# A polynomial in place of theta's logarithm on GpSimd, and memory-layer work cut into halves with second places in the order

## The chip, the cores and the metric

The kernel runs on one core of a Trainium2 chip. The core has five engines that matter here: TensorE (PE, matrix products; its weight loads are shown as PEld), VectorE (DVE), ScalarE (ACT), GpSimd (POOL) and SyncE (SP, which issues the transfers). The metric is the device time of one execution in microseconds, as the median of several runs.

## The reference

The input `x` is four sequences of 1024 rows of 256 numbers, in float32. Four layers follow each other, each added to what went in:

```python
x = x + attention(layernorm(x))      # 16 heads of 16, a second norm inside, softmax over 1024 keys
x = x + ffn(layernorm(x))            # one 256x256 product with weights of -1, 0, 1 times a scale
x = x + memory_layer(layernorm(x))
x = x + ffn(layernorm(x))
```

The memory layer makes keys, values and queries of width 64 by products and a causal convolution over four rows, and three numbers per row from the same input: alpha, eta (means of sigmoids) and theta, `(softplus(hidden @ tW.T + tb) * 0.1).mean(-1)`. Softplus is log(1 + exp(x)), computed here as max(x, 0) + log(1 + exp(-|x|)). In chunks of 128 rows, the gradient of a small two-layer network's loss is taken for each row at the state at the chunk's start, clipped in its norm, and two recurrences run over the rows, `S = eta * S - theta * g` and `W = (1 - alpha) * W + S`. What the network answers with each row's own `W` is multiplied with `Wo`, divided by the root of its mean square, and gated.

## The kernel before

**Blocks and units.** The attention runs over the queries in four blocks of 256 rows. Each block has eight units (a sequence and half of the heads), 32 in all, numbered u. A unit goes through eight turns, one for each 128 keys; the text writes turn 10.4 for the turn with the fifth keys of unit 10. A turn has two half-steps (`half`, with `pr` 0 and 1). In a half-step TensorE computes four matmuls of row maxima (`mx`, L244), for a unit ten turns ahead, then eight of scores (`sc`, L284) and two that subtract the maxima (L292). VectorE reduces `mx` (`nm`, L249) and ScalarE takes two exps of the scores (`pt`, L298). `weigh` (L312) multiplies the exps of the turn before with the values.

**PSUM.** `mx` has two buffers, the sums one, and the scores and every tile of side work share a ring of three (`mps`).

**Side work in lanes.** Everything else that can run beside the attention is a generator in one of the lanes settle, finish, theta, memory, ready, answers, last, outputs, before. `finish` makes the attention's output, its norm, and the first ffn of a pair of tiles (`po`, `hn`, `pf`, `hd`). When all tiles of a block are through, `theta` is started for each chunk of the block (two chunks), and `memory()` runs `prepare` (convolutions, eta, alpha, scans), `advance` (the gradient and the state) and `retrieve` (the answers) of the chunk, then starts `output` (product with `Wo`, gate, norm, last ffn, store). A generator yields where others may come between; the number that it yields is the time until it may go on, in turns of the written order (a half-step counts 0.5). `beside` is called once a turn, after the first half-step, and takes pieces from the lanes as long as a budget of TensorE columns lasts.

**What sets the order.** The order of TensorE, VectorE and ScalarE is the order in which the program emits the instructions, up to `by_hand.close()` behind the last unit. GpSimd's and SyncE's order is set by a scheduler, as is all of the tail (`rest`, `alone`), in which the last block's theta, memory layer and outputs run. An engine works through its own order and stands at an instruction whose input isn't there.

**Names that the change touches.** `theta`: `u` is exp(-|x|) (L507), the logarithm is the activation at L512, with the rounding of 1 + u put right by L509, L510 and a subtraction on GpSimd (L513); `thp` is the product that takes the mean. `prepare`: `vkps` and `qqps` are the projections (L559), `convolved` the convolution with one ScalarE and three VectorE operations, `natp` the transposed keys and values and `nat` their copy, the square of `nat` on GpSimd (L591, in the buffer named `ms`), `kk` its sum on VectorE (L596), `aeps`, `pa` and `pe` the numbers eta and alpha, L621 and L642 the scans on VectorE, `kqp` the product of keys and queries (L651) and `kqm` (L653) and `qq` (L654) what is made of it. `advance`: `zT`, `zn`, `prT`, `prn`, `da` are products of the gradient. `output`: `gps` the gate, `ops` the product with `Wo`, `o2` its copy, then squares, a reciprocal root (`rsi_o`, `rso_o`), the gating, the sum into `X`, statistics and norm of the result (`rsi_e`, `rso_e`, `nb_e`), the transposition `oth` and the last product `opf`. A norm is applied on ScalarE (L91), from a reciprocal root on GpSimd (L72) and a shift there (L84, L85).

In `output` the test `add is not V.tensor_add` holds in every call, since each access to `V.tensor_add` makes a new object: the last chunk's call takes the same branches as the others.

Of the kernel before, what the change touches and what calls it, by code (L numbers as in the profile page):

```python
# [13 lines left out]
ALU = mybir.AluOpType  # L14
# [12 lines left out]
D = 64  # L27
N5 = 512
EPS_LN = 1e-5

OWN = {mybir.EngineType.PE, mybir.EngineType.DVE, mybir.EngineType.Activation}

# [5 lines left out]
def tile_hybrid(ctx: ExitStack, tc: tile.TileContext, x, ln_gamma, ln_beta, w_qkv, b_qkv, w_out, b_out,  # L38
# [63 lines left out]
    def flat(t):  # L102
        return t.rearrange("p b t -> p (b t)")
# [350 lines left out]
    )}  # L454
    at = {"now": 0.0, "due": 0}

    def start(lane, gen, key=None):
        lanes[lane].append([gen, at["now"], key])

    def piece(lane):  # L460

        w = lanes[lane][0]
        n = taken[0]
        gap = next(w[0], None)
        used = taken[0] - n
        at["now"] += used / 1500
        if gap is None:
            lanes[lane].pop(0)
        else:
            w[1] = at["now"] + gap  # L470
        return used

    def beside(pace):

        at["due"] = min(at["due"] + pace, 1500)
        done = 0
        for lane in lanes:
            while lanes[lane] and lanes[lane][0][1] <= at["now"] and at["due"] >= 1 and done < 700:
                used = piece(lane)
                at["due"] -= used  # L480
                done += used
        return done

    def alone():

# [10 lines left out]
    def theta(k, cs):  # L496


        xh = xs_of[k][:, cs].rearrange("p c b t -> p (c b t)")
        m = cs.stop - cs.start  # L500
        u, w = (
            pools["lp"].tile([P, N5 // 2], F32, tag=f"th{name}", name=f"{name}_{k}_{cs.start}")[:, : 2 * m * P]
            for name in "uw"
        )
        V.scalar_tensor_tensor(out=u, in0=xh, scalar=-1.0, in1=xh, op0=ALU.mult, op1=ALU.min)
        yield 1
        A.activation(u, u, AF.Exp)  # L507
        yield 1
        V.tensor_scalar(w, u, 1.0, None, ALU.add)  # L509
        V.scalar_tensor_tensor(out=u, in0=w, scalar=-1.0, in1=u, op0=ALU.add, op1=ALU.subtract)  # L510
        yield 1
        A.activation(w, w, AF.Ln)  # L512
        G.tensor_sub(w, w, u)  # L513
        yield 1
        V.scalar_tensor_tensor(out=w, in0=xh, scalar=0.0, in1=w, op0=ALU.max, op1=ALU.add)
        yield 2
        ps = mps([P, m, 2, 2], f"thp_{k}_{cs.start}", 256)
        for c in range(m):
            for b in range(2):
                o = (2 * c + b) * P  # L520
                T.matmul(ps[:, c, :, b], lhsT=w[:, o : o + P], rhs=ot, start=True, stop=True)


        c0 = BLOCKS[k][0] // P + cs.start
        V.tensor_scalar(thn[:, c0 : c0 + m, :], ps.rearrange("p c h b -> p c (h b)"), -0.01, None, ALU.mult)
        yield 1
# [23 lines left out]
    def prepare(c, g, own):  # L550
# [12 lines left out]
        def convolved(what, w, cw):  # L563
            ps = projected(w, f"{what}ps")
            r = wk.tile([P, B, P + 3], F32, tag="w", name=f"r{what}_{c}")
            if c == 0:
                G.memset(r[:, :, 0:3], 0.0)
            else:
                G.tensor_copy(r[:, :, 0:3], carry[what])
            A.copy(r[:, :, 3:], ps)  # L570
            carry[what] = small.tile([P, B, 3], F32, tag=f"cy{what}", name=f"cy{what}_{c}", bufs=2)
            G.tensor_copy(carry[what], r[:, :, P : P + 3])
            y = own(what)
            A.activation(y, r[:, :, 0:P], AF.Identity, scale=cw[:, 0:1], bias=cw[:, 4:5])
            for j in range(1, 4):
                V.scalar_tensor_tensor(
                    out=y, in0=r[:, :, j : j + P], scalar=cw[:, j : j + 1], in1=y, op0=ALU.mult, op1=ALU.add
                )
            g[what] = y
            return y  # L580

        vk = convolved("vk", wvk, cw_vk)
        yield 1

        ps = mps(full, f"natp_{c}", 256)
# [5 lines left out]
        G.tensor_mul(sq, nat[:, :, D:], nat[:, :, D:])  # L591
        g["nat"] = nat
        yield 0
        qq = convolved("qq", wqq, cw_qq)
        kk = small.tile([P, B], F32, tag="kk", name=f"kk_{c}")
        V.tensor_reduce(kk, sq, AX.X, ALU.add)  # L596
        g["kk"] = kk
# [20 lines left out]
        V.memset(oma[:, :, 0:1], 0.0)  # L618

        def scan(dst, factor, added, r=slice(0, P)):  # L620
            V.tensor_tensor_scan(  # L621
                out=flat(dst)[r, :], data0=flat(factor)[r, :], data1=flat(added)[r, :], initial=0.0,
                op0=ALU.mult, op1=ALU.add,
            )

        scan(x1, eta, fe, slice(0, D))
        yield 1
        au1 = own("au1")  # L630
        scan(au1, oma, x1)
        au2 = own("au2")
        nc.sync.dma_start(au2[:D], au1[D:])
        nc.sync.dma_start(au2[D:], au1[:D])
        el = els[c % 2]
        with nc.allow_non_contiguous_dma(reason="a column"):
            nc.sync.dma_start(el[D:, :], x1[:D, :, P - 1])
        yield 1

        ls = own("dzw")  # L640
        for b in range(B):
            V.tensor_tensor_scan(  # L642
                out=ls[:, b, :], data0=eta[:, b, :], data1=ident, initial=0.0, op0=ALU.mult, op1=ALU.add
            )
        yield 1
        ms = own("ms")
        scan(ms, oma, ls)

        ps = mps(full, f"kqp_{c}", 560)
        for b in range(B):  # L650
# [174 lines left out]
    def output(c, box, groups, op, add):  # L825
# [23 lines left out]
        for p in pairs:  # L849
            ps = mps([P, 2, C], f"ops_{c}_{p.start}", 512)  # L850
            for e in range(2):
                T.matmul(ps[:, e, :], lhsT=ret[:, p.start + e, :], rhs=woT, start=True, stop=True)  # L852
            A.copy(o2[:, p, :], ps)
            for b in (p.start, p.start + 1):
                junk = pools["op"].tile([P, C], F32, tag="hT", name=f"junk_{c}_{b}")
                A.activation(junk, o2[:, b, :], AF.Square, accum_out=ss[:, b : b + 1])
            if p is pairs[1]:
                box.pop(("ret", c))
            yield 0
# [4 lines left out]
        for q in groups:  # L864
            for b in range(q.start, q.stop):
                o = b - q.start
                V.scalar_tensor_tensor(  # L867
                    out=gt[:, b, :], in0=o2[:, b, :], scalar=r[q.start][:, o : o + 1], in1=gt[:, b, :],
                    op0=ALU.mult, op1=ALU.mult,
                )  # L870
            add(X[:, q, c, :], X[:, q, c, :], gt[:, q, :])  # L871
            if add is not V.tensor_add:
                yield 2
            rn[q.start] = norm_stats([X[:, b, c, :] for b in range(q.start, q.stop)], q.stop - q.start, f"e{c}_{q.start}")
            yield 1
# [117 lines left out]
    with ExitStack() as by_hand:  # L993
        by_hand.enter_context(tc.manual_schedule(engines=OWN))
        share(m=8)
        with ExitStack() as s1_:
# [261 lines left out]
            def unit(u):  # L1258
                nonlocal late
                for kc in range(NT):  # L1260
                    if kc == 0:
                        load_keys(u + 1, range(1, 4))
                    if kc == 3:
                        if u + 2 < n0:
                            through("before", lambda key: key <= units[u + 2][1])
                        load_queries(u + 2)
                        load_keys(u + 2, (0,))
                        if u + 1 < U:
                            load_values(u + 1)
# [17 lines left out]
            def memory():  # L1287
                for k, (t0, w) in enumerate(BLOCKS[:-1]):
# [4 lines left out]
                    for c in range(c0, c1):  # L1293
# [11 lines left out]
            def rest():  # L1305
# [52 lines left out]
                start("ready", ready())  # L1358
                for c in cs:
                    if c + 1 < NT:  # L1360
                        start("outputs", output(c, box, [slice(0, B)], to_put(c), G.tensor_add))
# [93 lines left out]
```

## Time and profile before

| | |
|---|---|
| runs | 1477.01, 1477.69, 1477.88 us; median 1477.69 |
| the profiled execution's own time | 1477.84 us |
| its span | 1476.1 us |
| attention with the memory layer beside it | 457.6 to 1342.5 us, 884.9 us |
| tail | 1342.5 to 1476.1 us, 133.6 us |
| instructions on VectorE / ScalarE / GpSimd / SyncE, as built | 1642 / 1448 / 437 / 882 |

The profile is of one execution. A busy share near 1 with a granted clock (PEclk) below 1 means that TensorE works, but slower. Lines of a timeline give the start, the duration, the engine, the line of the program, the operation, out<-in with shapes, how many instructions are taken together, and in brackets the idle time before and what ended it. A group's line ends with busy time and mean duration in ns, then the idle time before and its releasers.

### The profile page before, as it was taken

The page shows a single profiled execution, that of the slowest core. Times are in us where ns is not written, and L with a number is a line of the kernel's source. Part 1 is how long each engine was busy: PE and PEld are TensorE (multiplying, and loading weights), DVE is VectorE, ACT ScalarE, POOL GpSimd, SP SyncE. Part 2 cuts the span into 40 slices and gives each one's busy share as a digit, 9 for nine tenths or more (in the row PEclk, how much of TensorE's full clock was granted, in tenths as well). Part 3 has the DMA queues.
Part 4 walks back from the last instruction along what each step waited for, and adds up shares of the span by engine and source line. Part 5 has one row for each costly group of instructions (what it writes and reads, how often), then busy time and mean ns, then how long its engine had stood idle before and what let it go on. Part 6 is the DMA issues. An engine that isn't in the chain of part 4 may idle for free. (4 is left out here: it accounts for less than half of the span.)

```text
span 1476.1 us, 32993 instructions
## 1 busy us (share of the span) xinstructions
PE 1356.1 (92%) x13568; PEld 843.4 (57%) x13568; DVE 1020.5 (69%) x1640; ACT 785.9 (53%) x1477; POOL 236.8 (16%) x432
## 2 busy tenths in 40 slices
PE   6589999999999999999998999999999999996886
PEld 4346555556555556565654565666556656664664
DVE  5766767587777766877778767776778677712653
ACT  2124636466666555656566655655665555553333
POOL 4431111000000200211011101210102102201232
PEclk9759989999999789999999999999999899988877
DMA  6605432533333221222233222223232022101000
GB/s 219 203 32 197 142 135 81 199 103 109 106 101 112 81 60 59 65 76 84 90 101 109 76 84 77 86 77 98 77 126 80 17 76 90 49 23 37 22 8 29
DMA packets 98211, 132.71 MB, mean 90 GB/s; under 512 B 27980, under 2 KB 70284, under 8 KB 98060
## 3 DMA queue, kind: packets, MB, share of 16 engines
q1 hardware_dynamic: 97788, 129.81, 27.6%
q8 instruction: 107, 1.75, 0.5%
q10 hardware_dynamic: 272, 0.79, 0.1%
q14 instruction: 44, 0.36, 0.1%
HBM read 89.69 MB, written 38.76 MB: 87 GB/s over the span
## 5 line engine op out<-in xcount | busy, mean ns | idle before, releaser
L298 ACT ACTIVATE pt<-sc 128x512 f32<-128x512 f32 x1024 | 555.2, 594 | 452.2 <-PE sc L292 451.6
L249 DVE TENSOR_REDUCE nm<-mx 128x2 f32<-128x1024 f32 x512 | 617.8, 1220 | 144.1 <-PE mx L244 126.1
L284 PE MATMUL sc<-q0slot,kslot 32*128 32x256 f32 x2048 | 373.4, 339 | 24.2 <-ACT pt L298 12.8
L312 PE MATMUL av<-pt,v 128*32 128x256 f32 x4096 | 310.6, 404 | 6.9 <-DVE a L320 6.2
L284 PE MATMUL sc<-q1slot,kslot 32*128 32x256 f32 x2048 | 309.7, 291 | 0.0
L244 PE MATMUL mx<-kslot,q0slot 32*128 32x512 f32 x1024 | 264.8, 516 | 24.3 <-DVE lo L1160 14.0
L284 PEld LDWEIGHTS sc<-q0slot,kslot 32*128 32x128 f32 x2048 | 239.1, 191 | 51.0 <-ACT pt L298 25.4
L244 PEld LDWEIGHTS mx<-kslot,q0slot 32*128 32x128 f32 x1024 | 98.2, 189 | 241.0 <-issue 117.2
L292 PE MATMUL sc<-mslot,ones_r 32*128 32x512 f32 x1024 | 232.5, 405 | 1.8 <-DMA mslot<-d 1.8
L284 PEld LDWEIGHTS sc<-q1slot,kslot 32*128 32x128 f32 x2048 | 233.8, 193 | 0.0
L244 PE MATMUL mx<-kslot,q1slot 32*128 32x512 f32 x1024 | 217.0, 422 | 0.0
L312 PEld LDWEIGHTS av<-pt,v 128*32 128x32 f32 x4096 | 99.2, 111 | 126.9 <-issue 88.8
L292 PEld LDWEIGHTS sc<-mslot,ones_r 32*128 32x128 f32 x1024 | 124.1, 193 | 2.5 <-DMA mslot<-d 2.4
L244 PEld LDWEIGHTS mx<-kslot,q1slot 32*128 32x128 f32 x1024 | 101.2, 195 | 0.0
L1155 PE MATMUL cps<-hT,wg 128*128 128x512 f32 x128 | 61.4, 626 | 0.0
L1160 DVE SCALAR_TENSOR_TENSOR lo<-cps,bqk,hi 128x512 fp32r<-128x512 f32 x32 | 23.9, 751 | 53.4 <-ACT hi L1159 45.4
L1159 ACT ACTIVATE hi<-cps,bqk 128x512 fp32r<-128x512 f32 x32 | 22.0, 687 | 49.9 <-PE cps L1155 24.8
L72 POOL TENSOR_TENSOR rso_hn<-rsi_hn,nhalf 128x2 f32<-128x2 f32 (+1 forms) x17 | 12.0, 708 | 223.1 <-DVE rsi_hn L71 196.8
L72 POOL TENSOR_TENSOR rso_hd<-rsi_hd,nhalf 128x2 f32<-128x2 f32 (+1 forms) x17 | 12.0, 703 | 187.4 <-DVE rsi_hd L71 170.1
L893 PE MATMUL opf<-ffn,ohT 128*128 128x256 f32 x128 | 35.1, 422 | 6.6 <-ACT ohT L888 6.6
L1155 PEld LDWEIGHTS cps<-hT,wg 128*128 128x128 f32 x128 | 24.3, 200 | 28.8 <-issue 26.6
L1196 POOL TENSOR_SCALAR X<-X,rr_a 128x256 f32<-128x256 f32 x32 | 18.5, 588 | 124.4 <-DVE h L1138 124.4
(361 smaller groups left out, 1662.4 us busy)
## 6 DMA issues: line engine op xcount, KB each, us to landing
kslot<-dk SPq DMA_DIRECT2D x64, 512.0 KB
v<-dv SPq DMA_DIRECT2D x32, 604.0 KB
q1slot<-dq SPq DMA_DIRECT2D x128, 64.0 KB
q0slot<-dq SPq DMA_DIRECT2D x64, 128.0 KB
da<-a SPq DMA_DIRECT2D x31, 256.0 KB
dv<-vtile SPq DMA_DIRECT2D x8, 604.0 KB
X<-in_L_attn_a_x_dram SPq DMA_DIRECT2D x8, 512.0 KB
dq<-hi SPq DMA_DIRECT2D x16, 256.0 KB
```

Of the source, the lines that this page charges most:

```text
L72: G.tensor_tensor(out=r[:, :n], in0=t[:, :n], in1=nhalf[:, :n], op=ALU.pow)
L244: T.matmul(ps[:, e, :], lhsT=qS[u][p][o : o + SL, j * P : (j + 1) * P], rhs=kt[o : o + SL, hf * N5 : (hf + 1) * N5], start=p == 0, stop=p ...
L249: V.tensor_reduce(nms[u][:, hf, 2 * pr : 2 * pr + 2, j], ps, AX.X, ALU.max, negate=True)
L284: T.matmul(ps[e][:, g * w : (g + 1) * w], lhsT=kS[u, g][o : o + SL, kc * P : (kc + 1) * P], rhs=qS[u][p][o : o + SL, g * w : (g + 1) * w], ...
L292: T.matmul(ps[e], lhsT=ones[o : o + SL, :], rhs=mslots[u % 2][o : o + SL, :], start=False, stop=True, skip_group_check=True,)
L298: A.activation(pt[:, e, :], ps[e], AF.Exp, scale=1.0 / HD**0.5)
L312: T.matmul(avs[u][SL * i : SL * (i + 1), part * w : (part + 1) * w], lhsT=v[:, kc, o : o + SL], rhs=pts[u, kc, i // 2][:, i % 2, part * w ...
L893: T.matmul(pf[:, e, :], lhsT=hT[:, cc, e, :], rhs=ffn[:, cc, :], start=cc == 0, stop=cc == 1)
L1155: T.matmul(ps, lhsT=wg[:, cc, n * P : (n + 1) * P], rhs=hT[:, cc, o], start=cc == 0, stop=cc == 1)
L1159: A.activation(high, ps, AF.Identity, bias=bqk[:, n : n + 1])
L1160: V.scalar_tensor_tensor(out=low, in0=ps, scalar=bqk[:, n : n + 1], in1=high.bitcast(F32), op0=ALU.add, op1=ALU.subtract,)
L1196: G.tensor_scalar(Xt, Xt, r[:, 6, t : t + 1], r[:, 7, t : t + 1], ALU.mult, ALU.add)
```

## The change

Three things are changed. In `theta`, for all but the last block, log(1 + u) is a polynomial of tenth degree without a constant term, evaluated on GpSimd in 18 operations in place, in three pieces, half a turn apart. In `prepare`, the convolutions and the scans are cut in two, and the second half may follow at a new place: a generator that yields a `Light` number may go on after a turn's second half-step, through `beside_light`, if it adds nothing to TensorE. In `output`, every chunk handles its four sequences in two groups of two, with squares, statistics and norms at separate places, and stores each group by itself.

As built, the counts of instructions become 1666 / 1432 / 574 / 889; TensorE's 10541 matrix instructions stay. On GpSimd, the polynomial of a block's first chunk stands ahead of the square of `nat` (L591), and that of its second chunk, with two of the outer products `al` (L548) in it, ahead of the reciprocal root and shift of `hd` (L72, L84, L85). On VectorE, the two halves of each scan follow one another in the same place. `kqp` and `zT` are in one place in all six chunks beside the attention.

```diff
+LOG1P = (
+    1.0, -0.49999904, 0.33330004, -0.24954559, 0.19678117, -0.15311863, 0.10614265, -0.0570642, 0.01990716, -0.00325638
+)
...
+    class Light(float):
+        pass
+
     def start(lane, gen, key=None):
-        lanes[lane].append([gen, at["now"], key])
+        lanes[lane].append([gen, at["now"], key, False])
...
         else:
-            w[1] = at["now"] + gap
+            w[1], w[3] = at["now"] + gap, isinstance(gap, Light)
         return used
...
+    def beside_light():
+
+        for lane, w in lanes.items():
+            if w and w[0][3] and w[0][1] <= at["now"]:
+                assert piece(lane) == 0
...
         A.activation(u, u, AF.Exp)
         yield 1
-        V.tensor_scalar(w, u, 1.0, None, ALU.add)
-        V.scalar_tensor_tensor(out=u, in0=w, scalar=-1.0, in1=u, op0=ALU.add, op1=ALU.subtract)
-        yield 1
-        A.activation(w, w, AF.Ln)
-        G.tensor_sub(w, w, u)
-        yield 1
+        if k == len(BLOCKS) - 1:
...
+        else:
+            G.tensor_scalar(w, u, LOG1P[-1], LOG1P[-2], ALU.mult, ALU.add)
+            for n, c in enumerate(LOG1P[-3::-1]):
+                G.tensor_mul(w, w, u)
+                G.tensor_scalar(w, w, c, None, ALU.add)
+                if n % 3 == 2:
+                    yield 0.5
+            G.tensor_mul(w, w, u)
+            yield 1
         V.scalar_tensor_tensor(out=w, in0=xh, scalar=0.0, in1=w, op0=ALU.max, op1=ALU.add)
...
             for j in range(1, 4):
+                if j == 2:
+                    yield Light(0)
                 V.scalar_tensor_tensor(
...
-        vk = convolved("vk", wvk, cw_vk)
+        vk = yield from convolved("vk", wvk, cw_vk)
...
-        qq = convolved("qq", wqq, cw_qq)
+        qq = yield from convolved("qq", wqq, cw_qq)
...
         def scan(dst, factor, added, r=slice(0, P)):
-            V.tensor_tensor_scan(
-                out=flat(dst)[r, :], data0=flat(factor)[r, :], data1=flat(added)[r, :], initial=0.0,
-                op0=ALU.mult, op1=ALU.add,
-            )
+            for o in (slice(0, 2), slice(2, 4)):
+                if o.start:
+                    yield Light(0)
+                V.tensor_tensor_scan(
+                    out=flat(dst[:, o])[r, :], data0=flat(factor[:, o])[r, :], data1=flat(added[:, o])[r, :],
+                    initial=0.0, op0=ALU.mult, op1=ALU.add,
+                )
...
-        scan(x1, eta, fe, slice(0, D))
+        yield from scan(x1, eta, fe, slice(0, D))
         yield 1
         au1 = own("au1")
-        scan(au1, oma, x1)
+        yield from scan(au1, oma, x1)
...
-        yield 1
+        yield 0.5
 
         ls = own("dzw")
         for b in range(B):
+            if b == 2:
+                yield Light(0)
             V.tensor_tensor_scan(
...
         ms = own("ms")
-        scan(ms, oma, ls)
+        yield from scan(ms, oma, ls)
+        yield 0
...
             A.copy(o2[:, p, :], ps)
+            if add is not V.tensor_add:
+                yield Light(0.5)
             for b in (p.start, p.start + 1):
...
             add(X[:, q, c, :], X[:, q, c, :], gt[:, q, :])
             if add is not V.tensor_add:
-                yield 2
+                yield Light(1.5)
             rn[q.start] = norm_stats([X[:, b, c, :] for b in range(q.start, q.stop)], q.stop - q.start, f"e{c}_{q.start}")
-            yield 1
+            yield 1 if add is V.tensor_add or q is groups[-1] else Light(0.5)
         for q in groups:
-            (norm_apply_here if q.start else norm_apply)(
+            (norm_apply_here if q.start and add is V.tensor_add else norm_apply)(
...
-            yield 2 if q is groups[-1] and add is not V.tensor_add else 0
+            if add is not V.tensor_add:
+                yield Light(0.5) if q is groups[0] else 2
+            else:
+                yield 0
...
+                        if pr == 1:
+                            beside_light()
...
-                        start("outputs", output(c, box, [slice(0, B)], to_put(c), G.tensor_add))
+                        start("outputs", output(c, box, [slice(0, 2), slice(2, 4)], to_put(c), G.tensor_add))
```

The last edit is made in `memory` and in `rest`.

More of the change, by code (lines that the diff above doesn't have):

```diff
@@ L508, in theta @@
         yield 1
-        V.tensor_scalar(w, u, 1.0, None, ALU.add)
-        V.scalar_tensor_tensor(out=u, in0=w, scalar=-1.0, in1=u, op0=ALU.add, op1=ALU.subtract)
-        yield 1
-        A.activation(w, w, AF.Ln)
-        G.tensor_sub(w, w, u)
-        yield 1
+        if k == len(BLOCKS) - 1:
+            V.tensor_scalar(w, u, 1.0, None, ALU.add)
+            V.scalar_tensor_tensor(out=u, in0=w, scalar=-1.0, in1=u, op0=ALU.add, op1=ALU.subtract)
+            yield 1
+            A.activation(w, w, AF.Ln)
+            G.tensor_sub(w, w, u)
+            yield 1
+        else:
[6 more added lines that the diff above has]
+            G.tensor_mul(w, w, u)
+            yield 1
         V.scalar_tensor_tensor(out=w, in0=xh, scalar=0.0, in1=w, op0=ALU.max, op1=ALU.add)
@@ L1360, in rest @@
                     if c + 1 < NT:
-                        start("outputs", output(c, box, [slice(0, B)], to_put(c), G.tensor_add))
+                        start("outputs", output(c, box, [slice(0, 2), slice(2, 4)], to_put(c), G.tensor_add))
                     else:
```

## The prediction

> **What bounds the kernel now.** I read the page's busy table first, then the clock row of its slices, the groups by shape, the timeline of ScalarE and GpSimd around the logarithm, and stretches of the span. TensorE is the bound; what can be won in the attention is its idle time and its half clock.
>
> ```profile
> PE 1356.1 (92%) x13568; PEld 843.4 (57%) x13568; DVE 1020.5 (69%) x1640; ACT 785.9 (53%) x1477; POOL 236.8 (16%) x432
> PEclk9759989999999789999999999999999899988877
> 457.60:1342.50 884.90, 841.92 (x9077) 529.66 (x9074) 630.51 (x959) 522.07 (x986) 123.80 (x229) 0.95 0.25 78
> 1342.50:1476.10 133.60, 98.59 (x448) 70.71 (x444) 67.13 (x165) 44.62 (x90) 39.51 (x61) 0.78 0.08 22
> ```
>
> The last two rows are stretches: start and end, length, busy time of TensorE, its weight loads, VectorE, ScalarE and GpSimd with counts, granted clock, DMA share, GB/s. The first is the attention with the memory layer beside it, the second the tail. TensorE is busy 95% of the first at a clock of 0.95, GpSimd 14%.
>
> ScalarE's timeline shows what a step costs, and what the logarithm costs:
>
> ```profile
> 342.78 1.09 ACT L298 ACTIVATE pt<-sc 128x512 f32<-128x512 f32 x2 [0.52 <-PE sc L292]
> 344.38 1.09 ACT L298 ACTIVATE pt<-sc 128x512 f32<-128x512 f32 x2 [0.51 <-PE sc L292]
> ...
> 481.91 1.28 ACT L512 ACT_TABLE_LOAD   x1
> 483.20 0.42 ACT L512 ACTIVATE w<-w 128x256 f32<-128x256 f32 x1
> 485.76 1.28 ACT L298 ACT_TABLE_LOAD   x1 [0.99 <-PE sc L292]
> 487.06 1.08 ACT L298 ACTIVATE pt<-sc 128x512 f32<-128x512 f32 x2
> 489.44 1.08 ACT L298 ACTIVATE pt<-sc 128x512 f32<-128x512 f32 x2 [1.30 <-PE sc L292]
> 492.04 1.09 ACT L298 ACTIVATE pt<-sc 128x512 f32<-128x512 f32 x2 [1.51 <-PE sc L292]
> ```
>
> The exps of a half-step without side work are 1.60 us apart (344.38 − 342.78). After the two table loads they are 2.60 apart (492.04 − 489.44): half clock.
>
> ```profile
> 484.25 0.58 PE L284 MATMUL sc<-q0slot,kslot 32*128 32x256 f32 x1 [1.24 <-ACT m L607]
> ...
> 484.20:497.90 13.70, 13.65 (x115) 7.12 (x115) 11.06 (x21) 6.87 (x12) 3.72 (x9) 0.50 0.11 21
> ```
>
> TensorE idled 1.24 us behind ScalarE's queue (its row at 484.25) and then ran this whole stretch at 0.50. Between 426 and 1345 us there are thirteen stretches at 0.50, together 89 us, 6.8 on average; each costs 6.8 × (1 − 1.60/2.60) = 2.6.
>
> GpSimd's rows price the polynomial, and two rows show what waits on that engine's order:
>
> ```profile
> L1196 POOL TENSOR_SCALAR X<-X,rr_a 128x256 f32<-128x256 f32 x32 | 18.5, 588 | 124.4 <-DVE h L1138 124.4
> L513 POOL TENSOR_TENSOR w<-w,u 128x256 f32<-128x256 f32 x8 | 5.9, 738 | 51.3 <-ACT w L512 51.3
> L591 POOL TENSOR_TENSOR ms<-nat 128x256 f32<-128x256 f32 x7 | 4.3, 613 | 30.4 <-ACT nat L589 30.4
> L596 DVE TENSOR_REDUCE kk<-ms 128x4 f32<-128x256 f32 x7 | 2.9, 414 | 1.9 <-POOL ms L591 1.9
> ...
> 985.85 2.07 ACT L91 ACTIVATE o<-X,nb_e,rso_e 128x256 f32<-128x256 f32 x4 [0.94 <-POOL nb_e L85]
> ```
>
> To find what the side work costs TensorE beyond its own matmuls, I priced each turn (two half-steps) of units 10 to 31 from turns that hold the same side work undisturbed: 3.19 without any, +1.54 for a group of eight projections or gates, +1.7 for `vkps` or `aeps`, +3.1 for `natp` with `qqps`, and so on. What a turn takes above its price is its excess, some 71 us in all. By place: 25.6 in the turns of the six logarithms (6.2, 3.6, 1.7, 3.8, 1.7, 8.6), 21.2 in the bursts of squares, statistics and norms in `output` (turns 15.3, 16.6, 17.1, 23.1, 25.0, 30.5), 15.9 in other memory-layer turns (11.1, 18.6, 19.0, 26.6, 29.2), the rest scattered.
>
> **The change, part by part.** The sum is against the profiled execution's own 1477.84 us, 0.15 above the median of the three runs.
>
> *The logarithm leaves ScalarE in six of eight calls.* Six activations, their table loads and six VectorE pairs go, and the excess of those turns with them: −25.6. Bounds 0 and −25.6; I take all of it, as the rows show nothing else late there. What is late next is the polynomial.
>
> *The polynomial on GpSimd.* Eighteen operations in place, each needing the one before: nine tensor_scalars at 0.588, nine products at 0.61 (the row `ms`) to 0.74 (the row `w`, same operands), 0.08 between dependent ones (0.588 and 0.61 rows stand so apart): 12.2 to 13.2 us per call. VectorE's scan of `ms` took 1.96 us at 1233.86, beside GpSimd's 1.27 us `qq` product, and 1.21 at 505.30 alone: two-input operations of the two engines slow each other. If the three of the `qq` convolution (0.75 each) hold the polynomial up for all their time, it takes up to 15.5. In the changed kernel's order on GpSimd all eighteen of a block's first chunk stand ahead of the square of `nat` (L591), and all eighteen of its second, with two `al` (0.77 each) between them, ahead of `rso_hd` and `nb_hd` (L72, L84, L85). Both are waited for:
>
> Wait A, per block. Clock starts at the last score matmuls of turn x.2's first half (468.69 in block 0). exp(u) ends at +1.9, the polynomial at +14.2 to +17.4, the square +0.6, then `kk` on VectorE (+0.5). VectorE works in the written order, so the next reduction of row maxima (L249, 1.22) ends at +16.4 to +19.6. There are two `mx` buffers; TensorE needs that one at turn x.5's first half, +13.8 (3.2 + 6.3 + 4.9 for turns x.2 to x.4, less 0.6). TensorE idles 2.6 to 5.8, middle 4.2, and a stretch of half clock (2.6) follows as after the other idles: 6.8.
>
> Wait B, per block, in turn x+1.3. exp(u) ends at +2.5, polynomial and two `al` take 13.6 to 14.8, `rso_hd` 0.73 and `nb_hd` twice 0.2 with gaps: +17.5 to +18.6. ScalarE comes to the norm `hd` (L91) at +11.1 (turns of 4.8 and 4.7, and 1.6 to the end of the exps) and stands; its exps stand behind it. After `hd` (1.15) and the first exp a score buffer comes free at +19.3 to +20.3, where TensorE, three buffers deep, wanted it at +13.8: idle 5.5 to 6.5, with blocking 7.4, middle 6.5, with the clock 9.1.
>
> Three blocks: 3 × (6.8 + 9.1) = +48. Bounds: 0, if both consumers come as late by then as the polynomial, and 3 × (5.8 + 7.4 + 2 × 5.3) = +71, with 13.7 us of half clock each as at 484.20. The middle is nearest to the stretches' mean.
>
> A rule that speaks against the change as well: the Trainium skill, page "SBUF — State Buffer", section "Who interferes with whom", says that GpSimd's only ports are a pair shared with VectorE under an exclusive lock. The two scans above agree with taking turns (0.75 us longer). By the rule the A waits alone would be 3 × 2.25 = 7 us dearer than with none, by the middle above half of that is in.
>
> *Squares, statistics, norms and output groups of two pairs.* The operations stay (one rsqrt of 1.0 becomes two of 0.72; one more store per chunk on SP's queue, where nothing waits for a store). Bursts of four activations (2.07 at 985.85, behind `nb_e`) become pairs with a half-step between. 21.2 can go; A pair still takes 1.15 (the two `hd` norms) where a half-step leaves ScalarE 0.51: 0.64 over, twice in each of six bursts, so 8 stays: −13. Bounds 0 and −21.
>
> *Convolutions and scans.* The `vk` and `qq` convolutions are really cut over two places; in the built order the two halves of each scan stand back to back on VectorE, so the scans are no more spread than before, and six more instructions a chunk cost what the fixed part of one is, under 0.1 each. But the places move: `kqp` and `zT` now fall into one slot in all six chunks. Of three slots where `kqp` shared one before, 29.2 (`kqp` and `zT`) had an excess of 3.05, and at 18.6 (`thp` and `kqp`) the exps waited 4.22, as the `m` buffers filled with tiles whose reader was far back; `kqp` alone had none. 15.9 goes, 6 × 3.05 = 18.3 comes: +2.4. Bounds −16 and +6 (3.67, the excess at 18.6, each).
>
> *Work that moves.* Priced side work of units 10 to 31 falls from 809.2 to 803.8 us, −5.4; the gates and output products of chunk 5 go to the tail, which is bound by a chain with TensorE at 98.6 of 133.6 us busy: +5 of the same. I take −0.4; bounds −5.4 and +5.
>
> Sum: −25.6 − 13 + 2.4 − 0.4 + 48 = +11; 1477.84 + 11.4 = 1489.
>
> **The rivals.**
> *Faster: the polynomial is hidden.* Consumers arrive late enough on their own. For it: GpSimd is 14% busy here. Against: the order, and 2.6 and 5.5 us short even at the low ends. −36.6, so 1441. It decides from the point where A and B together cost under 36.6/3 = 12.2 a block.
> *Faster, less: waits without the clock.* The idles stay at 2.6 and 5.5 and the clock isn't cut: 3 × 8.1 − 36.6 = −12.3, so 1466. For it: TensorE idled 1.01 us ahead of `natp` at 470.20 with no half clock behind it. Against: 1.24 us at 484.25 had 13.7 behind it. The page "TensorE: Matmul & The Clock Gate", section "What's actually happening", lets the clock halve after an idle window of about 3.4 us. The stretches are multiples of 3.4, but the trace shows them after shorter idles. By that rule A at its low end would pay nothing for the clock.
> *Slower still.* Each wait at its high end with 13.7 us of half clock, slots at 3.67: −25.6 − 13 + 6 − 0.4 + 71 = +38, 1516.
> *The change doesn't spread.* If the norms' bursts stay as the scans do, −13 is 0: 1502.
>
> **How the numbers follow.** Forecast 0.47 (1480 to 1505), hidden 0.08, waits without the clock 0.24, slower still 0.13, no spreading 0.08. Runs of one kernel lie 0.9 us apart, so 0.2%, 3 us, is about what can be told. Faster: 0.08 and four fifths of 0.24, 0.27; same 0.08, from that case's rest and the forecast's low edge; slower 0.65. The range leaves out the hidden case and the dearer half of the slower one: 1458 to 1513. The likeliest case's own range is 1480 to 1505.
>
> **What would show it.** Right: `kk` (L596) waits for GpSimd's `ms` by microseconds in turns 10.3, 18.3 and 26.3; ScalarE's `hd` (L91) waits for `nb_hd` in 11.5, 19.5 and 27.5, and the first exp after it for `hd`; half clock after each; no table load between 457 and 1342; GpSimd busy some 75 us more; the norms of `output` in twos; exps after `kqp` idle about 3 us. Wrong: `kk` and `hd` without idle ahead of them, or the logarithm's excess reappearing elsewhere, or a longer tail.

## The result and the profile after

The changed kernel takes 1519.6 us (median of six runs, 1512.6 to 1525.8) against 1477.8 for the kernel before: 1.028 times as long, 95% interval 1.025 to 1.031. The direction was forecast; the size was not. The forecast was 1489 with a range up to 1513, and the time lies above it. The profiled execution has a span of 1518.3 us. Ratios and intervals, here and below, are of runs in the faster of two states that the chip shows, so they can differ a little from the ratio of two medians.

The page of the changed kernel, busy times and the clock row:

```profile
PE 1382.0 (91%) x13568; PEld 858.1 (57%) x13568; DVE 1018.0 (67%) x1664; ACT 768.9 (51%) x1461; POOL 328.6 (22%) x569
PEclk9679979999998679989998879999998789899888
```

TensorE has the same 13568 matmuls as before and is busy 26 us longer, GpSimd 92 us longer. The clock row has new dips in the slices of units 10 and 11, 18 and 19, 26 and 27, the first two units of each block's memory layer; below, x stands for the first of the two. From unit 10 to the end of unit 30 the half-clock stretches sum to 167 us, against 85 before. Some of that is TensorE's idle; it is busy for 150 and 82 us of them, and at the forecast's 0.385 per microsecond the difference of 68 costs 26 us. TensorE's idle in the same units rises from 42.6 to 59.3 us, by 17. The two together make 43 us, and the spans differ by 42.

The chain of waits that was forecast is there. VectorE, GpSimd and TensorE around the end of the first polynomial (timelines; line numbers are those of the changed file: L616 is the square of `nat`, L621 `kk`, L253 the reduction of maxima, L95 a norm on ScalarE, L89 its shift):

```profile
486.19 0.72 POOL L536 TENSOR_TENSOR w<-w,u 128x256 f32<-128x256 f32 x1
486.88 0.61 POOL L616 TENSOR_TENSOR ms<-nat 128x256 f32<-128x256 f32 x1
...
487.52 0.42 DVE L621 TENSOR_REDUCE kk<-ms 128x4 f32<-128x256 f32 x1 [6.55 <-POOL ms L616]
487.86 1.22 DVE L253 TENSOR_REDUCE nm<-mx 128x2 f32<-128x1024 f32 x1
...
489.13 0.79 PE L248 MATMUL mx<-kslot,q0slot 32*128 32x512 f32 x2 [6.47 <-DVE nm L253]
```

`kk` stands 6.55 us for the square, which stands behind the polynomial's last product; the next reduction is behind `kk`, and TensorE stands 6.47 us for its buffer. It is the same for the `kk` of turns 18.4 and 26.4, to 0.01 us. Wait B, ScalarE in turn 11.5, TensorE behind it, and TensorE's clock after both waits and between them (windows; PE, PEld, DVE, ACT, POOL busy, then PEclk):

```profile
543.07 0.72 POOL L536 TENSOR_TENSOR w<-w,u 128x256 f32<-128x256 f32 x1
543.75 0.73 POOL L76 TENSOR_TENSOR rso_hd<-rsi_hd,nhalf 128x2 f32<-128x2 f32 x1
...
545.12 1.09 ACT L95 ACTIVATE hd<-X,nb_hd,rso_hd 128x256 f32<-128x256 f32 x2 [6.07 <-POOL nb_hd L89]
...
546.74 0.53 PE L288 MATMUL sc<-q0slot,kslot 32*128 32x256 f32 x1 [4.12 <-ACT pt L302]
...
485.40:499.10 13.70, 9.97 (x70) 5.32 (x70) 8.37 (x17) 3.90 (x7) 2.94 (x6) 0.50 0.04 11
512.70:533.20 20.50, 20.50 (x148) 13.52 (x143) 11.30 (x17) 7.23 (x15) 8.66 (x15) 0.50 0.15 48
546.80:563.90 17.10, 15.79 (x109) 9.84 (x109) 7.57 (x13) 6.61 (x12) 1.03 (x1) 0.50 0.14 36
```

The first window begins within wait A (TensorE is busy for 9.97 of its 13.7 us), the last behind wait B. The middle one follows no long wait (TensorE stood 0.57 us at 510.5): it holds `kqp` with `zT` and `hnT` with `zn`, and TensorE is busy for all of its 20.5 us. The totals of the waits (us, times, longest) say the same; three of each are waits B and A, the fourth `kk` stands in the tail and the other three `hd` wait 0.7 us each:

```profile
ACT hd L95 <- POOL nb_hd L89: 23.2, 6, 9.0
DVE kk L621 <- POOL ms L616: 21.2, 4, 6.6
```

The polynomial's rows by shape:

```profile
L533 POOL TENSOR_SCALAR w<-w 128x256 f32<-128x256 f32 x48 | 43.4, 904 | 4.2
L532 POOL TENSOR_TENSOR w<-w,u 128x256 f32<-128x256 f32 x48 | 34.9, 728 | 3.8
```

A product takes 0.73 us, as priced. The addition, a tensor_scalar with one operation, takes 0.90 us (0.85 where nothing disturbs it), not the 0.588 that the forecast took from a tensor_scalar with two. The first polynomial ran from 470.54 to 486.91, 16.4 us, where the sum had 12.2 to 15.5.

### The profile page after: what moved, and what is told of

It is laid out like the page before. It is cut to its first block, busy times and chain, and to the rows that moved or that the text cites. A ratio compares the mean times of both kernels' runs of the same rounds, so it can differ in the third digit from the quotient of the medians.

```text
span 1518.3 us, 33129 instructions
## 1 busy us (share of the span) xinstructions
PE 1382.0 (91%) x13568; PEld 858.1 (57%) x13568; DVE 1018.0 (67%) x1664; ACT 768.9 (51%) x1461; POOL 328.6 (22%) x569
## 3 DMA queue, kind: packets, MB, share of 16 engines
q1 hardware_dynamic: 97900, 129.81, 27.6%
## 4 chain that ended last, share of the span: by engine, by line
PE 68%; DVE 11%; POOL 8%; ACT 5%; DMA 3%; issue 2%; SPq 1%; DVEq 0%; ACTq 0%; POOLq 0%
PE av L316 14%; PE mx L248 12%; PE sc L288 10%; PE sc L296 7%; DVE nm L253 4%; PE cps L1191 3%; ACT pt L302 3%; POOL w L533 3%; POOL w L532 2%; PE vps L1214 2%; PE po L413 2%; PE gps L868 2%; PE opf L929 2%; PE pf L413 1%; PE tps L446 1%
## 5 line engine op out<-in xcount | busy, mean ns | idle before, releaser
L253 DVE TENSOR_REDUCE nm<-mx 128x2 f32<-128x1024 f32 x512 | 619.3, 1220 | 172.8 <-PE mx L248 145.8
L288 PE MATMUL sc<-q0slot,kslot 32*128 32x256 f32 x2048 | 380.8, 344 | 21.9 <-ACT pt L302 15.8
L316 PE MATMUL av<-pt,v 128*32 128x256 f32 x4096 | 315.0, 410 | 5.7 <-DVE a L324 5.6
L288 PE MATMUL sc<-q1slot,kslot 32*128 32x256 f32 x2048 | 317.4, 296 | 0.0
L248 PE MATMUL mx<-kslot,q0slot 32*128 32x512 f32 x1024 | 269.7, 527 | 42.8 <-DVE nm L253 27.7
L288 PEld LDWEIGHTS sc<-q0slot,kslot 32*128 32x128 f32 x2048 | 245.1, 194 | 45.2 <-ACT pt L302 25.6
L296 PE MATMUL sc<-mslot,ones_r 32*128 32x512 f32 x1024 | 238.5, 413 | 3.1 <-DMA mslot<-d 3.1
L288 PEld LDWEIGHTS sc<-q1slot,kslot 32*128 32x128 f32 x2048 | 240.6, 198 | 0.0
L248 PE MATMUL mx<-kslot,q1slot 32*128 32x512 f32 x1024 | 221.2, 431 | 0.0
L296 PEld LDWEIGHTS sc<-mslot,ones_r 32*128 32x128 f32 x1024 | 128.4, 198 | 4.0 <-DMA mslot<-d 3.8
L533 POOL TENSOR_SCALAR w<-w 128x256 f32<-128x256 f32 x48 | 43.4, 904 | 4.2
```

The source lines that it names most:

```text
L248: T.matmul(ps[:, e, :], lhsT=qS[u][p][o : o + SL, j * P : (j + 1) * P], rhs=kt[o : o + SL, hf * N5 : (hf + 1) * N5], start=p == 0, stop=p ...
L253: V.tensor_reduce(nms[u][:, hf, 2 * pr : 2 * pr + 2, j], ps, AX.X, ALU.max, negate=True)
L288: T.matmul(ps[e][:, g * w : (g + 1) * w], lhsT=kS[u, g][o : o + SL, kc * P : (kc + 1) * P], rhs=qS[u][p][o : o + SL, g * w : (g + 1) * w], ...
L296: T.matmul(ps[e], lhsT=ones[o : o + SL, :], rhs=mslots[u % 2][o : o + SL, :], start=False, stop=True, skip_group_check=True,)
L316: T.matmul(avs[u][SL * i : SL * (i + 1), part * w : (part + 1) * w], lhsT=v[:, kc, o : o + SL], rhs=pts[u, kc, i // 2][:, i % 2, part * w ...
L533: G.tensor_scalar(w, w, c, None, ALU.add)
```

## The experiments

They ran on chips where single runs of one kernel scatter by some 20 us (the kernel before: 1465 to 1489), so times are given as ratios to the runs of the kernel before on the same chip, whose median was 1471 to 1475. A turn's excess is its time above its price, found as in the prediction; sums of it are over units 10 to 30. The kernel before has 70.7 us by it, the changed one 115.1. As the prices are fitted to each trace, two excesses that differ by less than some 5 us can't be told apart.

**The changed kernel again.**

> The changed kernel itself, on the chip of the other experiments: 1.028 times the kernel before, 1516 us.

Ratio 1.023, interval 1.017 to 1.029. Wait A is the same (6.49 to 6.51 us of TensorE idle behind the three `kk`). Behind wait B TensorE idles 6.3, 7.2 and 7.4 us, where the first profile has 4.1, 7.2 and 4.1. Half clock sums to 140 us, 27 less than in the first profile, with 15 us less time. So the clock's share varies from run to run, and wait B with it; wait A doesn't.

**Halves with the logarithm.**

```diff
-        if k == len(BLOCKS) - 1:
+        if True:
             V.tensor_scalar(w, u, 1.0, None, ALU.add)
```

> The changed kernel with the logarithm back on ScalarE in all eight calls; halves, groups of two and places stay. Theory (the polynomial's place in GpSimd's order makes the loss): the excess of turns x.4 and x.5 (9.6 us a block) and of x+1.5 to x+1.7 (12.2 us a block) goes, 65 us, and the logarithm's 25.6 us come back: 1519.6 - 65 + 25.6 = 1480 us. Rival (the new places of the memory layer make the loss, the polynomial only lies beside it): above 1500 us.

Ratio 0.994, interval 0.991 to 0.998: faster than the kernel before, and 14 us below the expected 1480. Beside the attention `kk` doesn't wait for GpSimd, and `hd` only 0.7 us a time, 2.1 in all. Half clock is 75 us, excess 58.4. So the loss lies in the polynomial: 2.9% between this kernel and the changed one, some 42 us.

**The polynomial alone.** The kernel before with the new `theta` and nothing else.

> The kernel before with the polynomial alone; in its order the square of nat stands behind two of the eighteen operations of a block's first chunk, and rso_hd behind all eighteen of the second. Theory: no wait at kk, the logarithm's 25.6 us go, and the wait of hd costs up to 36 us over three blocks: between 1455 (hd not reached early) and 1490 us, with idle of ScalarE at hd as the sign; I expect 1485. Rival (the polynomial is harmless without the halves): 1452 us and no idle at hd.

Ratio 1.041, interval 1.035 to 1.048: 1535 us, much worse than expected and worse than the whole change. Beside the attention `kk` doesn't wait; the wait at `hd` is there, three times:

```profile
ACT hd L95 <- POOL nb_hd L89: 26.4, 3, 9.3
```

The excess of the turns of this wait is 39 us, near the 36 of the changed kernel. Another 20 us stand in turns 18.6, 21.4, 26.6 and 29.4, where `kqp` and `zT` now share a place, with 1.8 to 4.2 us idle each; before, they did so in 29.2 only. The written order moved when theta's steps did. The bursts of norms of the kernel before are still in this one. Of the 51 us by which the excess grew, a part is not assigned to a place, and of the 63 us between the two spans 7.5 stand in unit 31 and the tail.

**The square on VectorE.**

```diff
-        G.tensor_mul(sq, nat[:, :, D:], nat[:, :, D:])
+        V.tensor_mul(sq, nat[:, :, D:], nat[:, :, D:])
```

> The changed kernel with the square of nat on VectorE instead of GpSimd, so that kk waits for nothing on GpSimd. Theory: the 28.7 us of turns x.4 and x.5 go, less some 0.6 us a chunk of VectorE: 1491 to 1495 us, idle at hd as before. Rival (the next one that waits for GpSimd or the clock takes the time over): above 1510 us.

Ratio 1.006, interval 1.002 to 1.009, 1486 us: wait A goes and is not taken over by another. `hd` still waits:

```profile
ACT hd L95 <- POOL nb_hd L89: 29.8, 6, 9.2
```

Against 1.023 that is 1.7%, 26 us for A; the trace of the changed kernel has 28.7 in its turns.

**The second exp two turns later.**

```diff
-        yield 1
+        yield 1 if cs.start == 0 or k == len(BLOCKS) - 1 else 3
         A.activation(u, u, AF.Exp)
```

> The changed kernel with the exp of theta of each block's second chunk two turns later, which puts its polynomial behind rso_hd and nb_hd in GpSimd's order. Theory: the wait at hd goes and with it the 36.5 us of turns x+1.5 to x+1.7: 1483 us; the wait at kk stays. Rival (the polynomial then stands ahead of n or rso of the next pair and the time only moves): above 1505 us.

Ratio 1.020, interval 1.015 to 1.025: next to nothing gained. `hd` no longer waits for its shift, but theta's own last step does, on VectorE, with TensorE idle 7.0 to 8.6 us in turns x+1.7:

```profile
553.42 0.43 DVE L538 SCALAR_TENSOR_TENSOR w<-xs,w 128x256 f32<-128x256 f32 x1 [5.51 <-POOL w L536]
```

The rival was right that the time only moves, though to another instruction than it named, and the 1503 us fall just short of its 1505. That step can't be put off in this kernel: `finish` runs the theta lane to its end before the next block writes the buffer `xs`.

**A shorter polynomial by another form of the addition.**

```diff
-                G.tensor_scalar(w, w, c, None, ALU.add)
+                G.tensor_scalar(w, w, 1.0, c, ALU.mult, ALU.add)
```

> The changed kernel with the polynomial's additions as multiply by 1 and add, two operations in one tensor_scalar, in place of one. If the row of 0.85 us in the changed kernel belongs to the single operation, each costs 0.57 instead, and the polynomial 13.7 instead of 16.3 us: the idle at kk falls from 6.5 to 3.9 us a block and that at hd by 2.6: 15 us less or more with the clock, 1500 to 1505 us. If the row is VectorE's interference: 16.3 us again, 1519 us.

Ratio 1.012, interval 1.007 to 1.016, 1493 us. The addition with a second operation takes less than half the time of the one without:

```profile
L532 POOL TENSOR_TENSOR w<-w,u 128x256 f32<-128x256 f32 x48 | 37.5, 781 | 3.8
L533 POOL TENSOR_SCALAR w<-w 128x256 f32<-128x256 f32 x48 | 20.5, 427 | 4.2
```

`kk` waits 2.98 us where it waited 6.55 (turn 10.4, the same in the other two by TensorE's idle of 3.2), and `hd` waits 15.8 us in all, where it waited 23.2 and 29.7 in the two profiles of the changed kernel. So the 0.90 belongs to the form of the instruction, and the polynomial's length sets the waits.

**One operation in place of eighteen.**

```diff
-            G.tensor_scalar(w, u, LOG1P[-1], LOG1P[-2], ALU.mult, ALU.add)
-            for n, c in enumerate(LOG1P[-3::-1]):
...
-            G.tensor_mul(w, w, u)
+            yield 0.5
+            yield 0.5
+            G.tensor_scalar(w, u, LOG1P[0], None, ALU.mult)
             yield 1
```

> The changed kernel with the polynomial cut to its linear term, one operation in place of eighteen; it leaves out the logarithm's other terms, so theta is wrong, and everything else keeps its place. Theory (the length of the polynomial makes the loss): 1519.6 less 28.7 for kk and 36.5 for hd, 1454 us, and less than the kernel with halves and logarithm (1466). Rival (the loss lies in the halves and places): above 1490 us.

Four runs, at 1446, 1454, 1473 and 1474 us, beside a median of 1475 before. The loss is gone, so the length makes it. Whether a theta that costs next to nothing is faster than the one with the logarithm and its table loads (1466 us) these four don't tell, as they lie on both sides of it. In the profiles the excess is 58.3 us here and 58.4 there, and units 10 to 30 take 830 us here and 836 there: a gain of some 6 us there, not of 25.6.

**`kqp` and `zT` apart.** The kernel with halves and logarithm, and

```diff
         g.update(au2=au2, ms=ms, kqm=kqm)
-        yield 0
+        yield 1
```

> The kernel with halves and with the logarithm on ScalarE, and kqp and zT one turn apart in all six chunks (the memory layer's steps after kqp one turn later). Theory (two tiles of late readers in one place fill the ring of three): the 1.9 us idle and the half clock at turn x+1.2 go, some 6 us in each of three places and 2 to 4 in the other three: 1445 to 1450 us against 1466. Rival (the narrow memory products hold the clock down wherever they are): 1466 us again.

Ratio 0.993, interval 0.989 to 0.997, against 0.994 with the two together: nothing gained. The 1.9 us idle at x+1.2 fell to 0.9 to 1.1, but in units 11 and 19 the turn of `prT` and `prn` now stands behind the logarithm's two table loads on ScalarE, and TensorE idles 2.6 us there, with 7.5 and 7.2 us of the turn at half clock:

```profile
527.54 1.28 ACT L526 ACT_TABLE_LOAD   x1
528.83 0.42 ACT L526 ACTIVATE w<-w 128x256 f32<-128x256 f32 x1
529.27 1.28 ACT L726 ACT_TABLE_LOAD   x1
...
531.49 0.58 PE L288 MATMUL sc<-q0slot,kslot 32*128 32x256 f32 x2 [2.60 <-ACT pt L302]
```

So the run doesn't decide between my theory of a full ring and the rival's, that the clock falls wherever the narrow products stand: a new wait came in with the change of place. `zn`, alone in its turn in these two units, ran at full clock.

**Output alone.** The kernel with halves and logarithm, with `prepare` put back as it was.

> Only the part of the change in output and its second places: logarithm on ScalarE, convolutions, scans and places of the memory layer as before. Theory (bursts of norms cost 21 us and pairs 8): 13 us faster, 1462 us. Rival (the bursts are hidden, or the pairs' own waits cost as much): 1475 us.

Ratio 0.987, interval 0.982 to 0.992: 19 us faster than before by the ratio. The groups of two with second places are the part of the change that gains. The halves of convolutions and scans, with the places that they bring, cost: 0.994 against 0.987, some 10 us. The intervals overlap by 0.001, so this cost is likely and not certain.

**The polynomial in the first chunks only.** The changed kernel with the square on VectorE and

```diff
-        if k == len(BLOCKS) - 1:
+        if k == len(BLOCKS) - 1 or cs.start:
             V.tensor_scalar(w, u, 1.0, None, ALU.add)
```

> The changed kernel with the square of nat on VectorE and the logarithm on ScalarE for each block's second chunk, the polynomial for its first. Theory (only what waits for GpSimd costs): no idle at kk nor at hd from the polynomial; against halves with logarithm (1466) the excess of the first chunks' table loads goes (1.3, 2.4 and 3.7 us in turns x.4 and x.5): 1459 us. Rival (the polynomial costs beside others too, by the ports): 1470 us or more.

Ratio 0.990, interval 0.987 to 0.993, 1460 us as expected. Neither wait is there (`hd` waits 0.7 us a time, as with the logarithm). A polynomial on GpSimd does no harm that the time shows where nothing that waits stands behind it.

**Theta's steps moved for both chunks.**

```diff
+        gaps = (1, 1, 2, 1) if k == len(BLOCKS) - 1 else (2, 3, 2, 1) if cs.start else (3, 2, 1, 0)
-        yield 1
+        yield gaps[0]
         A.activation(u, u, AF.Exp)
...
-                G.tensor_scalar(w, w, c, None, ALU.add)
+                G.tensor_scalar(w, w, 1.0, c, ALU.mult, ALU.add)
...
             G.tensor_mul(w, w, u)
-            yield 1
+            yield gaps[1]
         V.scalar_tensor_tensor(out=w, in0=xh, scalar=0.0, in1=w, op0=ALU.max, op1=ALU.add)
-        yield 2
+        yield gaps[2]
...
         V.tensor_scalar(thn[:, c0 : c0 + m, :], ps.rearrange("p c h b -> p c (h b)"), -0.01, None, ALU.mult)
-        yield 1
+        yield gaps[3]
```

> The changed kernel with the polynomial in both chunks, its additions with two operations, and theta's steps moved so that two operations of the polynomial stand ahead of the square of nat and none ahead of rso_hd; kqp and zT come a turn apart by it. Theory: no idle at kk and hd; the second chunk's result is wanted at turn x+2.0, some 14 us after its exp, and waits up to 3 us there: 1460 to 1475 us. Rival (the wait goes to the next in line whatever is done): above 1490 us.

Ratio 1.013, interval 1.007 to 1.018: the rival. `kk` is free and `hd` but for 0.7 us a time, and in blocks 1 and 2 theta's last step is again wanted too early:

```profile
851.90 0.42 DVE L539 SCALAR_TENSOR_TENSOR w<-xs,w 128x256 f32<-128x256 f32 x1 [7.13 <-POOL w L537]
```

TensorE idles 9.7 us in each of these turns (19.6 and 27.6). In the odd chunks `kqp`, `zT`, `zn` and `prT` come in turns that follow each other at half clock, 11.5 us of excess three times. Between `hd` and the writing of `xs` there isn't the room for 14 us of GpSimd.

**What combines.** Output as in the experiment of output alone, `prepare` as before, the polynomial in first chunks only and with the two-operation addition.

> Output in pairs at second places, memory layer as before, polynomial only in each block's first chunk, with its additions in two-operation form; logarithm on ScalarE in the second chunks. Two operations of the polynomial stand ahead of the square of nat, none ahead of rso_hd. Theory (the gain of output and of the removed table loads add where nothing waits for GpSimd): 1459 less the first chunks' 4.7, 3.5 and 1.7 us, 1449 to 1453 us. Rival (no gain beside output alone): 1459 us.

Ratio 0.988, interval 0.984 to 0.993. It beats the kernel before and the changed one, but not output alone (0.987): the rival. What the first chunks' table loads cost there, 9.9 us by the expectation, is not seen as a gain in the times. The two profiles leave room for a part of it: units 10 to 30 take 819.3 us against 823.5, though the fitted excess is 58.2 against 57.2.

**How long the half clock lasts.** The kernel before with ten extra activations ahead of the exps of chosen turns:

```diff
+        if (u, kc, pr) in ((6, 3, 1), (13, 6, 1)):
+            for n in range(10):
+                A.activation(pts[u, kc, 0][:, 0, :], pts[u, kc, 0][:, 0, :], AF.Identity)
         for e in range(2):
             A.activation(pt[:, e, :], ps[e], AF.Exp, scale=1.0 / HD**0.5)
```

> The kernel before with ten extra activations of 128x512 (about 6 us of ScalarE) ahead of the exps in two places: turn 6.3, with nothing but attention in the turns behind it, and turn 13.6, with zT, zn, prT, prn and da in the turns behind it. Both make TensorE idle some 4 to 5 us. Theory (the half clock lasts until a window holds the attention's own matmuls only; products of the memory layer keep it down): about 3.4 to 7 us at half clock behind the first, 14 to 21 behind the second. Rival (the length follows the idle time): the same length behind both.

10.2 us at half clock behind both. The second probe has the turns 6.2, 13.7 and 24.3:

> The kernel before with ten extra activations of 128x512 ahead of the exps in turns 6.2, 24.3 (attention alone behind both) and 13.7 (prT, prn, da and ops behind it). TensorE idles about 4 us in each. Theory (a window that holds narrow products of the memory layer doesn't end the half clock): 7 to 10 us at 6.2 and 24.3, 14 or more at 13.7. Rival (the idle time alone sets it): the same at all three.

Its half-clock stretches behind the three idles (windows as above; idle of 5.5, 4.7 and 5.5 us in the turns):

```profile
354.60:368.30 13.70, 11.62 (x99) 6.52 (x99) 5.06 (x5) 6.79 (x13) 0.00 (x0) 0.50 0.03 8
634.50:644.70 10.20, 8.72 (x57) 6.22 (x57) 3.56 (x4) 4.06 (x8) 0.00 (x0) 0.50 0.16 52
1050.90:1061.10 10.20, 6.03 (x53) 3.54 (x55) 4.03 (x6) 6.62 (x12) 2.30 (x1) 0.50 0.04 14
```

13.7 with attention alone behind it, 10.2 with `prT`, `prn` and `da`, 10.2 with attention alone. The probes, one run each, don't support that the products of the memory layer lengthen a stretch. What they do show is the size: an idle of about 5 us brings 10 to 14 us of half clock, not 6.8; TensorE is busy for 6.0 to 11.6 us of it, as part of the idle lies within the stretch.

A count over all sixteen traces speaks the other way. I cut the half-clock stretches between 450 and 1345 us into the 3.4 us windows whose multiples they are, and ask which window was the last of its stretch. Of the windows in which TensorE is busy over 97% and fewer than two matmuls of `kqp`, `zT`, `zn`, `prT`, `prn`, `da`, `pa`, `pe`, `thp`, `tps` begin, 178 of 273 ended a stretch; of those with two or more, 9 of 107; of those with idle time, 1 of 102. This is a correlation; these products also stand where the waits are. What sets the length stays open.

## Why the prediction was right or wrong

The kernel was forecast slower for the right reason, and the time came out above the range, because four terms of the sum were too small: the two waits, the memory layer's places, and what was put at nothing for the rest. In microseconds, the prediction's sum beside the excess in the trace of the changed kernel:

| term | forecast | in the trace |
|---|---|---|
| logarithm's turns | −25.6 | −25.6 (none left) |
| bursts of `output` | −13 | −14.4 (6.8 left) |
| memory layer's places | +2.4 | +12.2 (15.9 goes, 28.1 comes) |
| wait A, three blocks | +20.4 | +28.7 |
| wait B, three blocks | +27.3 | +36.5 |
| scattered | 0 | +7 |
| work moved from the attention to the tail | −0.4 | −5.4, and −0.9 in unit 31 and tail |

The rows sum to +38 beside a difference of 42 in the spans; the rest is in the prices, which are fitted to each trace. Before the tenth unit the two traces differ by 0.2 us.

**Wait A** was the right mechanism at the right place with the right consequence. The idle was 6.5 us, above the 2.6 to 5.8 forecast. The step that failed is the price of nine tensor_scalars at 0.588 from a row with two operations; eight of the nine have one, and took 0.85 to 0.90. The run with the two-operation form brought the idle to 3.2, and so shows the cause. The clock's part was sized well: beside the idle, 3.1 us a block are left of the 28.7, where the forecast had 2.6. The slowing by VectorE was far smaller than its bound: the two additions beside the convolution of `qq` took 1.39 and 1.17 in place of 0.85, 0.9 us together, not 2.3. The Trainium skill's page "SBUF — State Buffer", section "Who interferes with whom", has the two engines exclude each other there; 0.9 us beside 2.25 us of convolution is less than exclusion for all of its time.

**Wait B** was named rightly, and the step that failed is the clock behind it. It took 7 us a block and not 2.6: the stretches are 17 to 20 us long, with TensorE busy for 15.7 to 15.8 of each. The half clock's term came from the mean of the stretches before (6.8 us), which mostly follow idles of one or two microseconds; the probes with 5 us of idle had 10 to 14. The idle was sized well where the turns ahead ran at full clock. It was 4.1, 7.2 and 4.1 us, beside a middle of 6.5: in blocks 0 and 2 half clock reached into the turns between theta's exp and `hd`, so that ScalarE came to `hd` 12.4 us after that exp began in block 0, and 9.3 in block 1. In the second profile the three idles were 6.3, 7.2 and 7.4.

**The memory layer's places** were priced by the idle of a ring of three that is full. In the odd chunks' slots (14.0, 22.0, 30.0) TensorE idles 0.5 to 0.6 us; what came in the turns behind them, and in x+1.2 to x+1.4, is half clock with TensorE busy, but for 1.8 us of idle in 27.2. The step that failed is the cause, and with it the price: half clock in place of idle. What makes it half clock stays open, as the run with the two products apart didn't decide it.

**The bursts of `output`** were right within 2 us, and output alone gained 1.3%, the one part that does.

**The logarithm's 25.6** was right as a difference of traces and wrong as a gain of its own. With the work in halves and the logarithm still there, its turns have an excess of some 13 us, and a theta of one operation has as much excess in all as that kernel, with units 10 to 30 only 6 us shorter. The prediction added both gains as if neither touched the other.

**The rivals.** Slower still, with its 13.7 us of half clock behind each wait, gave 1516 and came nearest; it was given 0.13. In part that is luck: it put the waits at +71, where the trace has +65, and the places, the scattered turns and the moved work at +6 together, where they made +13. Waits without the clock had its argument from one idle of a microsecond, and the argument against it was no better: the same wait of 1.24 us that had 13.7 us of half clock behind it in block 0 stands twice more in the trace of before, with full clock behind it for 12 and 19 us:

```profile
796.28 0.38 PE L284 MATMUL sc<-q0slot,kslot 32*128 32x256 f32 x1 [1.24 <-ACT m L607]
1106.95 0.38 PE L284 MATMUL sc<-q0slot,kslot 32*128 32x256 f32 x1 [1.24 <-ACT m L607]
...
784.00:808.40 24.40, 22.14 (x244) 12.34 (x242) 20.13 (x33) 16.96 (x28) 4.81 (x11) 1.00 0.14 37
1100.00:1120.00 20.00, 17.73 (x207) 10.45 (x206) 17.51 (x27) 13.51 (x22) 4.20 (x9) 1.00 0.17 46
```

No spreading is refuted by output alone, hidden by both waits.

## What to carry to other kernels

Before work is moved to an engine that looks idle, read the order on that engine and ask of each instruction behind the new work who waits for it in an order of its own: 14% busy meant nothing here, two short instructions behind 16 us did. Then price a wait of the bounding engine with what its clock does after an idle of that length, from several idles of that length, and price each instruction from a row of the same form, not only of the same shape. A change with several parts is worth taking apart: here one part had all of the gain, and the polynomial took it more than twice over.

## What the runs showed of the hardware

GpSimd's tensor_scalar on 128x256 in float32 took 0.43 us with two operations and 0.90 with one; a multiplication by one ahead of the addition halves the time. TensorE's clock went to half after an idle of 1.24 us in one place and not in two others, and stayed there for 10 to 14 us around 5 us of idle, 6 to 12 of them with TensorE busy again. The Trainium skill's page "TensorE: Matmul & The Clock Gate", section "What's actually happening", has the clock back after about 3.4 us of sustained work; here the stretches are multiples of 3.4 us, but the window 512.7 to 533.2 lasted six of them with TensorE busy throughout.
